# Constants, weight loads and a store of ones moved within the seam between two stages of a graph network

## The chip, the cores and the metric

The kernel runs on one core of a Trainium2 chip. The metric is the device time of one execution in microseconds. The core has five engines that run side by side, each through its own queue in order: PE (matrix multiply, into the accumulation banks of PSUM), DVE (vector work), ACT (scalar functions), POOL (general vector work) and SP, which here only issues transfers. The transfers themselves run on 16 DMA engines.

## The reference

There are 16 graphs of 1024 nodes with 128 features, an adjacency matrix of 1024 x 1024 for each, and a node mask. Two layers follow each other, each as `x = layernorm(x + layer(x))`.

- Layer 0 is a gated graph network: four times `m = adj^T (h W)`, then a GRU cell of `m` and `h`.
- Layer 1 first dilates the adjacency: row after row, every `sf`-th neighbour of a node with more than ten neighbours is removed, in both directions. Then three SAGE convolutions follow, each `out = (adj_d x / deg) Wr + x Wx + b`, rows divided by their norm, relu, and batch norm over all graphs and nodes. The three outputs, side by side, are multiplied by `Wl`.

## The kernel before, in words

The kernel runs in stages: the GRU and the dilation interleaved (classes `Gated` and `FixPoint`), then class `Sage` with `first` (first convolution, graph by graph), `second`, `third` and `last`. The batch norms join them, so that a convolution is only begun when the one before has seen all graphs. The adjacency kept by the dilation is stored as a bf16 matrix of what is not removed (`e_nr`), and layer 0's result as `e_sum`, both in device memory. The seam of this case lies between the first stage and `first`.

In `first` a graph is worked on in 16 slots. `slot(b, t)` runs slot `t` with two graphs in hand: the current one `b`, for the convolution, and the next one `n = b + 1`, whose adjacency is being formed. `b` starts at -1: in the sixteen slots of this lead-in turn nothing is convolved, and graph 0 is only prepared. A slot holds:

- `unit(n, t)`: one block of the dilated, transposed adjacency. PE adds up a half row of `p_nr` (L1482) and four blocks each of `p_a` (L1488) and `p_nr` (L1489) in PSUM, and ACT writes the result to `p_at` (L1490). Units 0 to 7 read the adjacency tiles a0 to a3 of the graph, units 8 to 15 read a4 to a7.
- `pack` (L1497): POOL turns the unit of the slot before into bytes, which SP stores for the later stages (`at8`, L1685 and L1677).
- `check` (L1506): DVE passes once over an adjacency tile, counts entries that aren't 0 or 1, and leaves bf16 values in the tile's lower halves. It stands in slots 4, 5, 10 and 11 for tiles 4 to 7 of graph `n`, and in slots 12 to 15 for tiles 0 to 3 of the graph after it.
- `norm_stats`, `norm` (L1527), `split_x` (L1405, L1406), `turn_x` (L1411): the layer norm of graph `n`'s rows `p_s`, their parts of high and low precision `p_xh` and `p_xl`, and their transpose.
- For graph `b`: `agg` (L1561, the adjacency times features, 8 matmuls each in slots 0, 1, 3, 4 and again 9, 10, 12, 14), `degrees`, `out_first` in slots 5 and 7 (with the weights `wr`, `wx` and the bias row `r6`), `scale_rows`, `rows`, and the stores.

The order of work on PE, DVE, ACT, POOL and SP is the written order of the program within a stage (a manual schedule), so a slot's place in the code is its place in every queue. SP issues all loads of this stage: `load_a` (L1458, one tile of 512 KB), `load_nr` (L1466, half a graph, 1 MB), `load_s` (L1472). In a slot they stand first: for the graph after `n`, `load_nr` in slots 4 and 6, `load_s` in slot 7, `load_a` of tiles 0 to 3 in slots 8 to 11, and of tiles 4 to 7 in slots 0 to 3 of the next turn. SP waits when the buffer isn't free: `p_a0` and `p_a1` hold four tiles each, `p_nr0` and `p_nr1` one graph each.

Three functions are concerned. `load_given` issues twenty transfers: three pairs of SAGE weights (`wr` L1248, `wx` L1249), `wl` (L1250), ten vectors into `vr` (L1253) and the node mask three times into a working tile named `p_rh` (L1257). `constants` forms small constant tiles on DVE and two selects on POOL (L1272), a copy of the identity with its first row changed (`drop`, L1284), and a tile of ones which SP stores three times as rows of `rho` (L1290). Identity copy, ones and a junk tile lie in a working tile named `p_rl`. `first_weights` takes the weights through PE once, `wr` with `drop` (L1297), splits the bias into `r6` (L1330 to L1337), and casts the node mask into `mask48` (L1303). `constants` runs at the end of slot (-1, 9), `first_weights` at the end of slot (0, 1). The tiles `wr2` and `wxp` get their values only between `first` and `second`; `mask48` is read in `last`.

Of the kernel before, what the change touches and what calls it, by code (L numbers as in the profile page):

```python
# [8 lines left out]
F32 = mybir.dt.float32  # L9
BF = mybir.dt.bfloat16  # L10
# [11 lines left out]
P = 128  # L22
B = 16
N = 1024
C = 128
NB = N // P
# [576 lines left out]
def make_consts(tc, one, wk, ps, nodemask):  # L603
    nc = tc.nc
    ident = one.tile([P, P], F32, name="ident")
    make_identity(nc, ident)
    ident_b = one.tile([P, P], BF, name="ident_b")
    nc.vector.tensor_copy(ident_b, ident)
    one_col = one.tile([P, 1], BF, name="one_col")
    nc.vector.memset(one_col, 1.0)  # L610

    nm = wk.tile([B, N], F32, name="nm_in")
    nc.sync.dma_start(nm, nodemask)
    pm = ps.tile([P, NB, B], F32, name="nm_ps")
    for k in range(NB):
        nc.tensor.transpose(pm[:, k, :], nm[:, k * P:(k + 1) * P], ident[:B, :B])
    mask = one.tile([P, NB, B], F32, name="mask")
    nc.vector.tensor_copy(mask, pm)

    t = wk.tile([P, NB, B], F32, name="nm_t")  # L620
    nc.vector.tensor_scalar(t, mask, 0.0, 4106.0, op0=ALU.is_equal, op1=ALU.mult)
    first = one.tile([P, NB, B], BF, name="first")
    nc.vector.tensor_scalar(first, t, -10.0, None, op0=ALU.add)
    return {"ident": ident, "ident_b": ident_b, "one_col": one_col, "mask": mask, "first": first}
# [292 lines left out]
class Gated:  # L917
# [24 lines left out]
    def bank(self):  # L942
        return self.ps6.tile([P, HF], F32, name="h_g")
# [180 lines left out]
    def run(self, steps):  # L1124

        streams = [self.stream(s) for s in range(2)]
        first, second = streams
        first.load_x(first.b)
        for j in range(NB):
            first.load_adj(first.b, j)  # L1130
        self.load_weights()
        next(steps)
        first.begin_rows(first.b)
        self.prepare()
        second.load_x(second.b)
        for j in range(NB):
            second.load_adj(second.b, j)

        first.begin(0)
        for n in range(9):  # L1140
            next(steps)
        for b0 in range(0, B, 2):
            for l in range(L0):
                for s in range(2):
                    st, ot = streams[s], streams[1 - s]
                    self.layer(st, l, self.beside(st, ot, l, s, b0, steps))
        last = streams[1]
        for f in range(2):
            last.finish(f)
        for _ in steps:  # L1150
            pass
# [45 lines left out]
class Sage:  # L1197
# [61 lines left out]
    def constants(self):  # L1259

        nc, ident, K = self.nc, self.cst["ident"], 3 * B
        const = self.const
        self.one16 = const([1, 1], 1.0, "s_one16", F16)

        self.sel01 = const([10, 3, 6], 0.0, "s_sel01")
        for i in range(3):
            nc.vector.tensor_copy(self.sel01[:, i, 3:], ident[:10, 3 * i:3 * i + 1].to_broadcast([10, 3]))
        self.ones = const([6, P], 1.0, "s_ones", BF)
        nc.vector.tensor_add(self.part6, ident[:6, 0:3], ident[:6, 3:6])
        self.part48 = const([K, 3], 1.0, "s_part48")  # L1270
        for base, m in ((0, 1), (B - 1, -1)):
            nc.gpsimd.affine_select(self.part48, self.part48, pattern=[[-m * B, 3]], compare_op=ALU.is_ge,  # L1272
                                    fill=0.0, base=base, channel_multiplier=m)
        nc.vector.tensor_add(self.graph, ident[:K, :B], ident[:K, B:2 * B])
        nc.vector.tensor_add(self.graph, self.graph, ident[:K, 2 * B:K])
        nc.vector.memset(self.r6[:, C:], 0.0)
        work = self.wk.tile([P, NB, C], F32, name="p_rl", bufs=1)

        mask, junk = self.cst["mask"], work[:, 0, :].rearrange("p (a b) -> p a b", a=NB)
        nc.vector.scalar_tensor_tensor(junk, mask, 0.0, mask, op0=ALU.is_gt, op1=ALU.not_equal,  # L1280
                                       accum_out=self.bad[:, BAD - 1:BAD])

        drop = work[:, 1, :]
        nc.vector.tensor_copy(drop, ident)  # L1284
        nc.vector.memset(drop[:1, :], -1.0)
        nc.vector.memset(drop[:1, :1], 0.0)
        o = work[:B, 4:, :].bitcast(BF).rearrange("p a b -> p (a b)")
        nc.vector.memset(o, 1.0)
        for i in range(3):
            nc.sync.dma_start(self.rho[:, 3 + i, :], o)  # L1290
        self.drop = drop

    def first_weights(self):
        nc, ident = self.nc, self.cst["ident"]
        bank = lambda: self.ps1.tile([P, 4, P], F32, name="s_tr")[:, 0, :]
        w = bank()
        nc.tensor.matmul(w, self.drop, self.wr[:, 0, :], start=True, stop=True)  # L1297
        nc.vector.tensor_copy(self.wr[:, 0, :], w)
        v = bank()[:, :10]
        nc.tensor.transpose(v, self.vr, ident[:10, :10])  # L1300
        nc.vector.tensor_copy(self.vt, v)
        self.weights(0, bank()[:6, :])
        nc.vector.tensor_copy(self.mask48, self.m48)  # L1303

    def const(self, shape, v, name, dt=F32):
        t = self.one.tile(shape, dt, name=name)
        self.nc.vector.memset(t.bitcast(F32) if dt is FR else t, v)
        return t
# [106 lines left out]
    def first(self):  # L1415

        nc, tc, cst = self.nc, self.tc, self.cst
        with ExitStack() as c:
            pool = lambda name, **k: c.enter_context(tc.tile_pool(name=name, **k))

            self.atp = [pool("p_at0", bufs=1)]
            self.sp = pool("p_s", bufs=2)
            xp = pool("p_x", bufs=1)
            self.wk = pool("p_wk", bufs=2)
            self.atp.append(pool("p_at1", bufs=1))
            self.nrp, self.ap = [], []
            for i in range(2):
                self.nrp.append(pool(f"p_nr{i}", bufs=1))
                self.ap.append(pool(f"p_a{i}", bufs=4))
            self.ps1 = pool("p_ps1", bufs=1, space=PSUM)  # L1430
            self.ps2 = pool("p_ps2", bufs=2, space=PSUM)

            self.ps3 = pool("p_ps3", bufs=3, space=PSUM)
            c.enter_context(tc.manual_schedule(engines={ET.PE, ET.DVE, ET.Activation, ET.Pool, ET.SP}))
            self.g = {}
            self.load_nr(0, 0)
            for k in range(4):
                self.load_a(0, k)
            self.load_nr(0, 1)
            self.load_s(0)  # L1440
            for k in range(4, NB):
                self.load_a(0, k)
            self.load_given()
            self.eps = self.const([P, 1], 1e-5, "s_eps")
            self.less2 = self.const([P, 1], -2.0, "s_less2")

            self.xh = xp.tile([P, NB, C], FR, name="p_xh")
            self.xl = xp.tile([P, NB, C], FR, name="p_xl")
            for t, v in ((self.xh, 1.0), (self.xl, 0.0)):
                nc.vector.memset(t[:, :, :1].bitcast(F32), v)  # L1450
            for b in range(-1, B):
                for t in range(16):
                    self.slot(b, t)
# [146 lines left out]
    def slot(self, b, t):  # L1600

        nc, g, n = self.nc, self.g.get(b), b + 1
# [80 lines left out]
        if nxt:  # L1683
            if t == 10:
                nc.sync.dma_start(self.at8[n, 0], self.g[n]["b", 0])  # L1685
            if t == 13:
                nc.sync.dma_start(self.x1[n], self.g[n]["s"])
        if (b, t) == (-1, 9):
            self.constants()
        if (b, t) == (0, 1):  # L1690
            self.first_weights()
        if t == 1 and b >= 1:
            for f in range(2):
# [346 lines left out]
```

## Time and profile before

| | us |
|---|---|
| three runs | 2393.73, 2396.82, 2397.0 |
| span of the profiled execution | 2393.6 |
| PE busy in it | 2269.3 (95%) |
| DVE busy | 1924.3 (80%) |
| ACT busy | 1373.5 (57%) |
| POOL busy | 1014.7 (42%) |
| first transfer of the first SAGE stage issued at | 1316.73 |
| first unit's matmul at | 1328.39 |
| first aggregation at | 1366.89 |

Times in the text are microseconds from the start of the profiled execution. An engine's busy share says little by itself; what counts is which wait ended last at a given place. The granted TensorE clock is given as a share of full speed (0.98 over the whole span); its value in a stage matters where PE has stood still. "L1284" is line 1284 of the kernel, and names such as `p_a` are tiles, without their buffer numbers. The matmuls of a group overlap, so a group's time is from its first start to its last end.

### The profile page before, as it was taken

The numbers are of one execution on the slowest core, as the hardware profiler recorded it, in microseconds if no ns is written. First come the engines' busy times: TensorE is split into PE (matmuls) and PEld (weight loads), VectorE is DVE, ScalarE is ACT, GpSimd is POOL, SyncE is SP. The second block draws the span as 40 slices with busy tenths as digits, with TensorE's granted clock in tenths as the row PEclk, the third lists the DMA queues.
The fourth block names the chain that finished last, engine by engine and source line by source line (L and its number), as shares of the span: only waits on it lengthen the run. The fifth ranks groups of instructions, "written<-read, shape, count | busy, mean of one in ns | idle before, by whom it ended". The sixth has DMA issues, their size and how long they took to land.

```text
span 2393.6 us, 35727 instructions
## 1 busy us (share of the span) xinstructions
PE 2269.3 (95%) x11945; PEld 1561.1 (65%) x11945; DVE 1924.3 (80%) x4130; ACT 1373.5 (57%) x3209; POOL 1014.7 (42%) x963
## 2 busy tenths in 40 slices
PE   6999999999999999999999599999999889998987
PEld 4666555656556656656666377777777777776865
DVE  4998998989989989989899777877777466665876
ACT  3556565665565656565746466566666444545756
POOL 3235253353362543533622356666666344441001
PEclk9999999999999999999999799999999999999999
DMA  7337254364271553533630868777877366664414
GB/s 260 111 98 262 69 191 146 115 230 132 95 246 60 176 185 119 186 132 119 231 101 31 315 237 295 280 258 282 300 277 269 116 215 232 242 207 147 143 45 134
DMA packets 214394, 436.18 MB, mean 182 GB/s; under 512 B 59574, under 2 KB 80728, under 8 KB 214200
## 3 DMA queue, kind: packets, MB, share of 16 engines
q1 hardware_dynamic: 186756, 345.96, 41.9%
q0 software_dynamic: 23040, 83.90, 10.2%
q10 hardware_dynamic: 4400, 3.95, 0.5%
q8 instruction: 96, 1.57, 0.3%
q14 instruction: 102, 0.80, 0.1%
HBM read 324.49 MB, written 109.25 MB: 181 GB/s over the span
## 4 chain that ended last, share of the span: by engine, by line
PE 58%; DVE 16%; ACT 10%; DMA 9%; issue 4%; POOL 3%; SPq 0%; DVEq 0%; ACTq 0%; POOLq 0%
PE h_g L1092 15%; PE h_g L1080 12%; PE p_ag L1561 9%; DMA e_sum<-h_x 3%; DVE f_rank L735 3%; ACT s_junk L1389 3%; PE q_ag L1800 3%; PE p_u L1482 2%; PE p_u L1489 2%; PE p_u L1488 2%; DMA h_a<-in_adj_dram 2%; PE q_ob L1764 2%; PE s_tr L1411 1%; DVE s_o L1382 1%; PE u_p L1890 1%
## 5 line engine op out<-in xcount | busy, mean ns | idle before, releaser
L1092 PE MATMUL h_g<-h_h,h_wh 128*128 128x512 f32 x768 | 397.7, 599 | 3.4 <-DVE h_r L1105 3.3
L1092 PE MATMUL h_g<-h_ms,h_wi 128*128 128x512 f32 x768 | 392.2, 592 | 0.0
L1497 POOL CAST p_b<-p_at 128x512 uint8<-128x512 f32 x256 | 251.7, 1003 | 139.8 <-ACT p_at L1490 131.3
L735 DVE TENSOR_TENSOR_SCAN f_rank<-f_a,f_first,f_pd 128x1024 f16<-128x1024 f32 x128 | 299.1, 2342 | 3.3
L1080 PE MATMUL h_g<-h_a,h_hi 128*128 128x512 f32 x1024 | 284.8, 418 | 6.4 <-DMA h_a<-in_adj_dram 6.3
L1490 ACT ACTIVATE p_at<-p_u,s_less 128x512 fp32r<-128x512 f32 x256 | 175.7, 687 | 160.0 <-PE p_u L1489 155.1
L1092 PEld LDWEIGHTS h_g<-h_ms,h_wi 128*128 128x128 f32 x768 | 145.6, 190 | 183.9 <-issue 161.6
L1121 POOL TENSOR_TENSOR h_h<-h_zh,h_r 128x512 f32<-128x512 f32 x126 | 182.0, 1444 | 194.9 <-DVE h_r L1120 172.8
L1080 PE MATMUL h_g<-h_a,h_lo 128*128 128x512 f32 x1024 | 264.2, 395 | 0.0
L1080 PEld LDWEIGHTS h_g<-h_a,h_hi 128*128 128x128 f32 x1024 | 188.4, 188 | 71.0 <-issue 20.1
L863 DVE SCALAR_TENSOR_TENSOR f_nr<-f_u,f_q,f_a 128x1024 bf16<-128x1024 f16 x128 | 183.7, 1451 | 57.2 <-ACT f_u L912 50.6
L1115 POOL TENSOR_TENSOR h_zh<-h_z,h_h 128x512 f32<-128x512 f32 x63 | 80.4, 1276 | 323.8 <-ACT h_z L1111 323.8
L1080 PEld LDWEIGHTS h_g<-h_a,h_lo 128*128 128x128 f32 x1024 | 190.0, 188 | 39.3
L1506 DVE SCALAR_TENSOR_TENSOR p_a<-p_a 128x1024 bf16<-128x1024 f32 x128 | 209.4, 1674 | 3.1 <-DMA p_a<-in_adj_dram 3.1
L1092 PEld LDWEIGHTS h_g<-h_h,h_wh 128*128 128x128 f32 x768 | 129.1, 190 | 86.6 <-issue 67.3
L1389 ACT ACTIVATE s_junk<-s_o 128x128 bf16<-128x128 f32 x384 | 113.7, 298 | 109.3 <-DVE s_o L1382 109.3
L1083 ACT COPY h_ms<-h_g 128x512 f32<-128x512 f32 x128 | 73.7, 576 | 175.2 <-PE h_g L1080 131.2
L1108 ACT ACTIVATE h_r<-h_r,h_bi 128x512 f32<-128x512 f32 x128 | 92.3, 721 | 138.7 <-DVE h_r L1107 138.7
L1488 PE MATMUL p_u<-ident_b,p_a 128*128 128x128 bf16 x1024 | 144.7, 221 | 13.8 <-DMA p_a<-in_adj_dram 13.8
L909 ACT ACTIVATE f_u<-f_rank,f_q 128x128 f16<-128x128 f16 (+7 forms) x128 | 110.6, 867 | 75.2 <-DVE f_rank L849 75.2
L1489 PE MATMUL p_u<-ident_b,p_nr 128*128 128x128 bf16 x1024 | 144.7, 221 | 0.0
L1764 PE MATMUL q_ob<-s_wxp,q_xt 128*128 128x256 f32 x512 | 130.8, 399 | 0.0
(258 smaller groups left out, 4956.8 us busy)
## 6 DMA issues: line engine op xcount, KB each, us to landing
h_a<-in_adj_dram POOLq DMA_DIRECT2D x128, 512.0 KB, 7.4
p_a<-in_adj_dram SPq DMA_DIRECT2D x128, 512.0 KB
f_a<-in_adj_dram SPq DMA_DIRECT2D x124, 512.0 KB
e_nr<-f_nr SPq DMA_DIRECT2D x128, 256.0 KB
p_nr<-e_nr SPq DMA_DIRECT2D x32, 1024.0 KB
s_at<-p_b SPq DMA_DIRECT2D x32, 512.0 KB
s_ag<-s_ag SPq DMA_DIRECT2D x64, 256.0 KB
q_agi<-s_ag SPq DMA_DIRECT2D x32, 512.0 KB
```

What stands on the lines that cost most here:

```text
L735: nc.vector.tensor_tensor_scan(out, a, other[:, 0, 0:1].to_broadcast([P, N]), start, op0=ALU.add, op1=ALU.bypass)
L863: nc.vector.scalar_tensor_tensor(nr, self.us[g], self.q[:, 2, g:g + 1], self.a[g], op0=ALU.not_equal, op1=ALU.is_ge)
L1080: nc.tensor.matmul(pm[f], part[:, j, :], st.adj[j][:, half[f]], start=(j == 0 and n == 0), stop=(j == NB - 1 and n == 1))
L1092: nc.tensor.matmul(pg, lhs, rhs, start=(i == 0), stop=(i == len(mm) - 1))
L1121: aid.tensor_tensor(h, zh, r, ALU.subtract)
L1389: self.nc.scalar.activation(junk, o[:, i, :], AF.Square, accum_out=ss[:, i:i + 1])
L1488: nc.tensor.matmul(pu[:, i * P:(i + 1) * P], a[:, blk, 1], ib, start=False, stop=False)
L1489: nc.tensor.matmul(pu[:, i * P:(i + 1) * P], nr[:, k, blk], ib, start=False, stop=(i == 3))
L1497: self.nc.gpsimd.tensor_copy(g["b", f][:, j, :], g["at"][:, j, f * HF:(f + 1) * HF].bitcast(F32))
L1506: self.nc.vector.scalar_tensor_tensor(low, a, 0.0, a, op0=ALU.is_gt, op1=ALU.not_equal, accum_out=self.bad[:, c:c + 1])
L1561: self.nc.tensor.matmul(pa, hi[:, j, :], at[:, j, f * HF:(f + 1) * HF], start=(start and n == 0), stop=(stop and n == len(js) - 1))
L1764: nc.tensor.matmul(pb[:, i], g["xt"][:, f, blk], self.wxp, start=False, stop=(i % 2 == 1))
```

## The change

`constants` is called before the slots begin, and no longer at the end of slot (-1, 9). Its junk tile lies in `wxp`, its identity copy in `wr2`, its ones in the first 16 rows of `mask48`. Its stores of ones go to the end of slot (-1, 15). `load_given` is called at the end of slot (-1, 11), behind the loads of graph 1, and no longer before the slots. `first_weights` is called at the end of slot (0, 3), and no longer (0, 1).

```diff
     def constants(self):
...
-        work = self.wk.tile([P, NB, C], F32, name="p_rl", bufs=1)
-
-        mask, junk = self.cst["mask"], work[:, 0, :].rearrange("p (a b) -> p a b", a=NB)
+
+        mask, junk = self.cst["mask"], self.wxp[:, 0, :].rearrange("p (a b) -> p a b", a=NB)
...
-        drop = work[:, 1, :]
+        drop = self.wr2
         nc.vector.tensor_copy(drop, ident)
         nc.vector.memset(drop[:1, :], -1.0)
         nc.vector.memset(drop[:1, :1], 0.0)
-        o = work[:B, 4:, :].bitcast(BF).rearrange("p a b -> p (a b)")
-        nc.vector.memset(o, 1.0)
-        for i in range(3):
-            nc.sync.dma_start(self.rho[:, 3 + i, :], o)
-        self.drop = drop
+        nc.vector.memset(self.mask48[:B, :], 1.0)
 
     def first_weights(self):
...
-        nc.tensor.matmul(w, self.drop, self.wr[:, 0, :], start=True, stop=True)
+        nc.tensor.matmul(w, self.wr2, self.wr[:, 0, :], start=True, stop=True)
...
     def first(self):
...
-            self.load_given()
             self.eps = self.const([P, 1], 1e-5, "s_eps")
             self.less2 = self.const([P, 1], -2.0, "s_less2")
...
                 nc.vector.memset(t[:, :, :1].bitcast(F32), v)
+            self.constants()
             for b in range(-1, B):
                 for t in range(16):
                     self.slot(b, t)
...
     def slot(self, b, t):
...
-        if (b, t) == (-1, 9):
-            self.constants()
-        if (b, t) == (0, 1):
+        if (b, t) == (-1, 11):
+            self.load_given()
+        if (b, t) == (-1, 15):
+
+            for i in range(3):
+                nc.sync.dma_start(self.rho[:, 3 + i, :], self.mask48[:B, :])
+        if (b, t) == (0, 3):
             self.first_weights()
```

## The prediction

> **What bounds the kernel now.** I read four views in this order: the page's slices, the chain that ended last around the change, SP's own queue there, and the waits with the busy times by stage.
>
> The change touches one place: the seam between the GRU/dilation stage and the first SAGE pass. In the page's slices the seam is slice 23 (59.84 us each, so 1316 to 1376 us), the only one in which PE falls to 5 tenths. The chain says what ended last there (columns: start, us, what):
>
> ```profile
> 1320.67 12.89 DMA p_s<-e_sum
> ...
> 1344.23 5.27 DVE p_a L1506 x6
> 1350.88 5.23 DVE p_rl L1284
> 1356.62 0.92 DVE p_rl L1288
> 1359.84 6.85 DMA p_a<-in_adj_dram
> 1367.13 3.52 PE p_ag L1561 x8
> ```
>
> PE waits for graph 1's fourth adjacency tile. Its load was issued late because SP stood behind the stores of ones, which stood behind DVE's constants (L1284, L1288). SP's queue, in order of time:
>
> ```profile
> 1326.34 1.02 SPq L1248 DMA_DIRECT2D s_wr<-in_L_gnn_Wr_dram  x1
> 1328.52 0.33 SPq L1249 DMA_DIRECT2D s_wx<-in_L_gnn_Wx_dram  x1
> 1332.29 0.33 SPq L1248 DMA_DIRECT2D s_wr<-in_L_gnn_Wr_dram  x1
> ...
> 1344.56 1.24 SPq L1257 DMA_DIRECT2D p_rh<-in_nodemask_dram  x3
> 1345.84 0.97 SPq L1466 DMA_DIRECT2D p_nr<-e_nr  x2
> 1346.85 0.50 SPq L1472 DMA_DIRECT2D p_s<-e_sum  x1
> 1347.47 1.14 SPq L1458 DMA_DIRECT2D p_a<-in_adj_dram  x2
> 1357.56 1.25 SPq L1290 DMA_DIRECT2D s_rho<-p_rl  x3
> 1358.91 0.37 SPq L1458 DMA_DIRECT2D p_a<-in_adj_dram  x1
> ```
>
> Two delays stand in one queue: twenty weight loads from 1326.34 to 1345.84 ahead of everything of graph 1, then the stores of ones at 1357.56. The waits of 1290 to 1440 us give their prices, and the stages what the machine did meanwhile (span, PE, PEld, DVE, ACT, POOL busy, clock, DMA share, GB/s):
>
> ```profile
> PE p_u L1488 <- DMA p_a<-in_adj_dram: 13.8, 4, 6.1
> ...
> SPq L1290 <- DVE p_rl L1288: 8.9, 1, 8.9
> ...
> 1340.00:1347.00 7.00, 6.74 (x72) 5.19 (x70) 7.00 (x11) 5.67 (x11) 6.46 (x7) 0.90 0.26 69
> ...
> 1357.50:1366.70 9.20, 1.18 (x6) 0.39 (x6) 6.14 (x11) 0.00 (x0) 0.00 (x0) 0.50 0.76 248
> ...
> 1392.40:1426.10 33.70, 33.26 (x273) 26.22 (x273) 25.64 (x61) 20.82 (x50) 22.03 (x20) 1.00 0.76 281
> ```
>
> The DMA engines idle from 1340 to 1347 (69 GB/s) while small loads go out, and pay for it in 1357.5 to 1366.7, where PE has 1.18 us of work. From 1392.4 on a graph takes 33.7 us with PE busy 33.26: there the loop is PE's, and whatever shift the seam gives is carried to the end.
>
> **What the Trainium skill says.** "SBUF — State Buffer", section on the two separate sides: VectorE and GpSimd share a port pair as an exclusive lock, and an fp32 SBUF-to-SBUF copy takes it. The trace agrees: the 128x128 copy L1284 took 5.30 us and ended 0.1 us after POOL's last cast, and the same size without POOL beside it (L1323) takes 0.28:
>
> ```profile
> 1347.75 1.76 DVE L1506 SCALAR_TENSOR_TENSOR p_a<-p_a 128x1024 bf16<-128x1024 f32 x1
> ...
> 1350.80 5.30 DVE L1284 COPY p_rl<-ident 128x128 f32<-128x128 f32 x1
> ...
> 1346.57 3.37 POOL L1497 CAST p_b<-p_at 128x512 uint8<-128x512 f32 x2
> ...
> 1353.74 2.27 POOL L1497 CAST p_b<-p_at 128x512 uint8<-128x512 f32 x4
> ```
>
> "DMA: Bandwidth & Descriptors", section on the anatomy of one DMA: about 2 us fixed per DMA, mostly completion, so small transfers must overlap. Here the ten vectors and three mask rows go out 0.25 to 0.6 us apart with eight in flight, so each took under some 3 us, which agrees. "TensorE: Matmul & The Clock Gate", part 1: an idle window of about 3.4 us halves the clock. Here it shows 0.50 in the hole, and slot (0,0)'s eight matmuls take 3.76 us against 2.09 for the same eight at 1405.59.
>
> **Part 1: constants moved in front.** Today DVE is in them from 1349.43 to 1357.46, 8.03 us. Of these 5.30 is the locked copy. In front, POOL runs no elementwise work between 1322.6 and 1338.3, so the copy costs 0.28 and the group 8.03 - 5.30 + 0.28 = 3.0 us. They follow the two memsets of L1450 (1325.6). From there to 1333.59, where DVE waits for the first p_s tile, DVE has 8.0 us and uses 2.07 (three of 0.69): 5.9 us free for 3.0. If some fall ahead of the last GRU operations (L1121, L1058), p_u starts up to 3 us later. That is hidden too: after p_at of units 0 and 1 and the table load (done 1333.1) ACT waits 3.9 us for p_mv, which waits for p_s. Cost on the path 0, with 0 to 3 as bounds. POOL's two selects (0.59 us) go along, into idle time. What is gained is that DVE is out of the way at 1349.4.
>
> **Part 2: load_given moved behind graph 1's loads.** SP runs at most eight loads ahead: the 14th after the seam (second s_wr) waits for the 6th (p_nr), the 15th for the 7th (p_s, 1333.59), the 16th to 19th for the four a tiles (1336.48 to 1340.98). So the 12th to 14th become p_nr of graph 1 (two of 1 MB) and p_s (0.5 MB), issued at about 1326.4, 1328.5 and 1332.3, queued behind graph 0's tiles. They arrive in that order now, so I take it that graph 0 isn't slowed. Then a(1,0) to a(1,2): their buffers are free once unit (0,7) is through (1342.6) and checks 0 to 2 (1342.6). Then the byte store at8, which waits for POOL's pack of unit 7 (1348.2, the first of the two casts at 1346.57), then a(1,3) at about 1348.7. By volume: 2 + 0.5 + 2 + 0.5 MB = 5.24 million bytes after 1340.9, at the 415 GB/s seen before, are 12.6 us: a(1,3) lands at 1353.5 to 1354. It lands at 1366.7 today. **Gain at this point 12.7 to 13.2 us.**
>
> **Part 3: the twenty loads in their new place.** They are issued from 1349.1. The first seven wait in turn for the loads eight before, up to a(1,3) (1353.9); the other thirteen took 4.9 us (1340.98 to 1345.84): last at 1358.9. Then x1's store, the three of ones (1.25 us) and a(1,4) at about 1361.7: by chance the time at which it is issued now (1361.69). Landing about 1364.5, the last of the four about 1369.5; DVE's check needs the first at 1364 to 1370, PE the last in slot (0,8) at about 1376. p_nr and p_s of graph 2 follow by 1376, before slot (1,0). No cost, 2 us at the most.
>
> **Part 4: stores of ones from mask48.** Source ready since part 1, so SP no longer waits the 8.9 us. In return L1303's cast of the node mask into mask48 must wait for them (landed about 1363.6); DVE gets there at 1367 to 1370. Cost 0.
>
> **Part 5: first_weights from slot (0,1) to (0,3).** Same work, 1.6 us on PE (1373.81 to 1375.38) and a chain of 3.8 us on DVE. Its weights land by about 1360, PE arrives at about 1364. The row r6 must be ready for slot (0,5): one slot (2.7 us) and a unit (0.65) lie between, against 3.0 us from the first copy to r6: 0, at most 1.
>
> **Part 6: what takes the gap's place.** DVE's six checks (0,6) to (1,3) now run alone after 1357.46 (1.27 us each). Moved to 1349.5 they run beside POOL's remaining casts and alternate with them, 1.76 as above, one of 2.4 beside the split: about 11.5 us, to 1361, where uncontended they would end at 1357. norm_stats (2.2) then ends at 1363.3, the degree row and norms follow, first_weights finds DVE at 1366.7 where PE came at about 1364.6. That gives back about 2 us. Against it, PE stands still 2.5 us and not 16, so slots (0,0) and (0,1) may run warm: 1.6 + 0.6 us less. I take -2 for the first and 1 for the second.
>
> **Sum:** 12.9 - 2 + 1 = 12 us less, 2393.6 to 2381.6 in the profiled span. The runs shown are 2393.73 to 2397.0, median 2396.82; 12 off the median is 2385.
>
> **The rivals.**
> *Partial gain.* DVE beside POOL, or SP's small loads, end last in slots (0,1) to (0,6). For it: 1.76 against 1.27 us, and L1248's wait of 3.4 us. If the checks take 2.4 each (the worst seen) the end is 1364, three more lost, and with 2 us of late loads 5 to 8 us are left: 2389 to 2392. Against: PE has about 11 us of own work before it needs what DVE makes.
> *No change.* The loads queue but don't move earlier: graph 1's buffers in fact free late, or early p_nr takes bandwidth from p_s. Then a(1,3) still lands near 1366: 2395 to 2397. Against: p_nr of graph 1 is the first tile in its own pool, and the loads at 1321.55 had already waited for the dilation's last DVE instruction.
> *Slower.* PE takes its queue in order, so first_weights in slot (0,3) holds it until the last vector has landed. Place: twenty loads now stand between a(1,3) and that point. Price: 1 us for each us after 1364.6. They lasted 19.5 us when each waited for a large load; from 1349.1 that is 1368.6 plus landing, 5 lost. It decides against the change from 1377 on, 28 us for the twenty; at 33 us PE goes on at 1382.1, 17.5 lost against 12, and the time is 2402. Against: only seven have a large load eight places ahead.
>
> **How the numbers follow.** Forecast case 0.64 (2382 to 2388), a still warmer PE included; partial 0.22; no change 0.07; slower 0.07. Within 0.2% (4.8 us) is about what a measurement of this kernel can't tell from no change. Faster 0.86, same 0.07, slower 0.07. The range 2380 to 2392 holds the forecast and the partial case and leaves out the other two (0.14) and a tail; the forecast's own is 2382 to 2388.
>
> **What would show it.** Right: the a tile's 6.1 us wait on PE is gone and the fourth block of unit (1,0) starts at about 1354; DMA above 400 GB/s from 1340 to 1353; the copy of the identity at about 0.3 us before 1334; the checks of 1349 to 1361 at about 1.8 us. Wrong: a PE wait for s_wr or s_vr in slot (0,3), a(1,3) issued after 1352, the constants beside POOL's work, or p_s of graph 0 landing after 1335.

## The result and the profile after

The changed kernel takes 2385.58 us (median of four runs, 2382.49 to 2386.91), the kernel before 2396.60 in the same series: 0.9955 of its time, interval 0.9938 to 0.9972. That is 11.0 us less, against a forecast of 12. The profiled spans are 2393.6 and 2385.2, only 8.4 apart: the profiled execution of the changed kernel was the slowest of its four.

In the chain that ended last (start, us, what), the piece of 6.85 us for graph 1's tile and DVE's constants ahead of it are gone:

```profile
1321.20 12.50 DMA p_s<-e_sum
...
1344.49 4.40 DVE p_a L1501 x5
...
1354.52 5.76 DVE p_a L1501 x7
1360.29 0.77 DVE p_st L1510 x4
...
1365.27 1.12 DVE p_s L1522 x4
1368.80 2.98 PE p_ag L1556 x8
```

From 1354.52 to 1366.4 the chain now runs over DVE, but for 0.8 us of ACT: the checks, the statistics and the norm of graph 1. SP's queue (start, us, line, transfer) shows the new order and how the large loads are spread:

```profile
1326.65 4.34 SPq L1461 DMA_DIRECT2D p_nr<-e_nr  x2
1332.48 5.60 SPq L1467 DMA_DIRECT2D p_s<-e_sum  x1
1343.48 1.29 SPq L1453 DMA_DIRECT2D p_a<-in_adj_dram  x3
1348.56 0.33 SPq L1680 DMA_DIRECT2D s_at<-p_b  x1
1349.00 0.37 SPq L1453 DMA_DIRECT2D p_a<-in_adj_dram  x1
1349.42 0.71 SPq L1248 DMA_DIRECT2D s_wr<-in_L_gnn_Wr_dram  x1
...
1359.00 1.65 SPq L1688 DMA_DIRECT2D s_rho<-s_mask  x3
1360.76 1.31 SPq L1453 DMA_DIRECT2D p_a<-in_adj_dram  x3
```

Graph 1's `p_nr` and `p_s` are issued from 1326 to 1338 and no longer at 1345, its fourth tile at 1349.00 and no longer at 1358.91. The waits of 1290 to 1440, then the stages (span, PE, PEld, DVE, ACT, POOL busy, clock, DMA share, GB/s):

```profile
PE p_u L1483 <- DMA p_a<-in_adj_dram: 2.3, 1, 2.3
...
1340.00:1347.00 7.00, 6.66 (x62) 5.42 (x60) 7.00 (x12) 5.13 (x10) 5.57 (x8) 0.74 1.04 397
1357.50:1366.70 9.20, 7.00 (x52) 4.93 (x50) 8.36 (x33) 3.12 (x6) 6.77 (x8) 1.00 0.78 237
1392.40:1426.10 33.70, 33.22 (x273) 26.22 (x273) 25.73 (x64) 20.81 (x50) 22.41 (x21) 1.00 0.78 282
```

PE's 13.8 us of waits for tiles have become 2.3. The DMA engines move 397 GB/s where they moved 69, and in the old hole PE works 7.00 us of 9.20 where it worked 1.18. The later loop is as it was.

To compare executions I use one length, the seam: from the start of the first memset of `first` (`s_eps`) to the first aggregation of slot (0,9). It is 79.91 us before (1312.50 to 1392.41) and 68.65 after (1312.90 to 1381.55), 11.3 less. The gain is kept: the last `p_oa` product of the first convolution comes 577.1 us after that memset before, and 566.2 after, 10.9 less. A seam is read from one profiled execution; two more of the changed kernel, below, gave 68.91 and 68.01.

### The profile page after: what moved, and what is told of

Same layout as the page of the kernel before. It is cut to its first block, busy times and chain, and to the rows that moved or that the text cites. A ratio compares the mean times of both kernels' runs of the same rounds, so it can differ in the third digit from the quotient of the medians.

```text
span 2385.2 us, 35712 instructions
## 1 busy us (share of the span) xinstructions
PE 2272.1 (95%) x11928; PEld 1566.9 (66%) x11945; DVE 1921.6 (81%) x4130; ACT 1373.1 (58%) x3209; POOL 1018.7 (43%) x963
## 4 chain that ended last, share of the span: by engine, by line
PE 56%; DVE 17%; ACT 11%; DMA 8%; issue 4%; POOL 2%; SPq 0%; DVEq 0%; ACTq 0%; POOLq 0%
PE h_g L1092 14%; PE h_g L1080 11%; PE p_ag L1556 9%; DVE f_rank L735 3%; DMA e_sum<-h_x 3%; ACT s_junk L1384 3%; PE q_ag L1799 2%; DMA h_a<-in_adj_dram 2%; PE p_u L1483 2%; PE p_u L1484 2%; PE p_u L1477 2%; PE q_ob L1763 2%; PE s_tr L1406 1%; PE u_p L1889 1%; DVE s_o L1377 1%
## 5 line engine op out<-in xcount | busy, mean ns | idle before, releaser
L1492 POOL CAST p_b<-p_at 128x512 uint8<-128x512 f32 x256 | 257.1, 1024 | 123.2 <-ACT p_at L1485 123.2
```

The source lines that it names most:

```text
L1492: self.nc.gpsimd.tensor_copy(g["b", f][:, j, :], g["at"][:, j, f * HF:(f + 1) * HF].bitcast(F32))
```

## The experiments

Each expectation was written before its run. Theory: the tile's wait was set by two things in a row, SP's weight loads in front and DVE's locked copy in front of the stores. Rival: one of the two made nearly all of it.

**The loads moved, the constants left.** All of the change but `constants`, which is back at the end of slot (-1, 9) with its stores:

```diff
-            self.constants()
             for b in range(-1, B):
...
-        if (b, t) == (-1, 15):
+        if (b, t) == (-1, 9):
+            self.constants()
             for i in range(3):
                 nc.sync.dma_start(self.rho[:, 3 + i, :], self.mask48[:B, :])
```

> The changed kernel, but with the constants and the stores of ones back at the end of slot (-1, 9); only the weight loads (and first_weights) are moved. Theory (two delays in series in SP's queue, the later one decides): the first three quarters of graph 1's loads go out early, but the third a tile still waits on SP for the stores of ones, which wait for the 5.3 us copy; a(1,2) is issued near 1358.9 and a(1,3) near 1359.8, now into idle DMA engines, so it lands near 1363 to 1364. Gain against before 2.5 to 3.5 us, time 2393 to 2394. Rival (the weight loads in front are the main piece, the DMA engines' idle 7 us is what is won): 7 us or more, time 2389 or less.

2392.0 us, 0.9987 of before (0.998 to 0.9994); seam 75.29. The gain of 3.7 is a little more than the 2.5 to 3.5 expected, and it came by another path: the copy was not slow here, and the third tile went out at 1354.16 and not near 1358.9. First DVE, then SP, then the chain, then two stages:

```profile
1350.95 0.21 DVE L1283 COPY s_wr<-ident 128x128 f32<-128x128 f32 x1
...
1352.53 4.93 DVE L1500 SCALAR_TENSOR_TENSOR p_a<-p_a 128x1024 bf16<-128x1024 f32 x1
...
1352.62 1.43 SPq L1685 DMA_DIRECT2D s_rho<-s_mask  x3
...
1355.18 6.32 DMA p_a<-in_adj_dram
...
1344.00:1348.00 4.00, 3.76 (x45) 2.84 (x43) 4.00 (x7) 3.67 (x7) 3.09 (x2) 1.00 0.95 369
1348.00:1353.00 5.00, 2.76 (x33) 1.98 (x31) 4.60 (x22) 3.10 (x6) 4.54 (x8) 0.99 0.04 15
```

Here the copy took 0.21 us, just ahead of POOL's row of casts (from 1351.16), and the check after it took 4.93. Even so, SP stood behind the stores' source until 1352.6, and with all that was issued before already in, the DMA engines stood nearly empty (15 GB/s) for 5 us; the last two tiles were issued after it.

**The constants moved, the loads left in front.**

```diff
                 self.load_a(0, k)
+            self.load_given()
             self.eps = self.const([P, 1], 1e-5, "s_eps")
...
-        if (b, t) == (-1, 11):
-            self.load_given()
```

> The changed kernel, but with the weight loads back in front of the slots; only the constants, their stores and first_weights are moved. Theory: graph 1's loads start at 1345.8 as before and are then bound by volume (5.24 million bytes at 0.4 per us are 13 us), so a(1,3) lands near 1359.5 to 1360 in place of 1366.7; DVE's checks end near 1361, before PE needs them. Gain 6 to 7.5 us, time 2389 to 2391. Rival (weight loads the main piece): 4 us or less, time 2392.5 or more.

2391.85 us, 0.9985 (0.9976 to 0.9993); seam 77.65. Expected was 6 to 7.5 less, measured 3.9. Chain and stages:

```profile
1349.43 13.51 DMA p_a<-in_adj_dram
...
1346.00:1348.00 2.00, 1.89 (x26) 1.41 (x24) 2.00 (x3) 1.73 (x4) 2.00 (x3) 1.00 0.67 195
1348.00:1363.00 15.00, 3.01 (x26) 1.51 (x25) 7.93 (x12) 2.08 (x4) 8.57 (x9) 0.62 1.02 385
```

The tile was issued at 1349.43, which is 37.4 us after the seam's start against 36.1 in the changed kernel, and landed 13.5 us later. Two terms were missing from the expectation: the DMA engines were at 195 GB/s until 1348, and the store of `x1` (0.5 MB, issued 1350.91) shared them with the tile. 11 half-megabyte units (5.77 million bytes) at 385 GB/s are 15.0 us: 1348 to 1363. Here volume ends last, not issue. A gain of 4 us or less was the rival's mark for this run; what speaks against the rival is that the loads alone didn't give its 7 us either.

**One instruction of the kernel before: the identity copy on ACT.**

```diff
-        nc.vector.tensor_copy(drop, ident)
+        nc.scalar.copy(drop, ident)
```

> The kernel before with one line changed: the copy of the identity in the constants runs on ACT in place of DVE, so that it doesn't take part in the lock with POOL. Theory: DVE's 5.3 us copy is on the path; the stores of ones go out near 1352.5, a(1,3) near 1355, volume-bound as in the constants-alone kernel: a(1,3) lands near 1359.5 to 1361. Gain 5 to 7 us, time 2390 to 2391.5. Rival (the copy only looks long, DVE would wait elsewhere, for instance the stores wait for POOL or the memset takes the lock's time): 0 to 1 us, time 2396.

2392.11 us, 0.9985 (0.9978 to 0.9991); seam 75.46. 3.6 us less; 2390 to 2391.5 was expected. DVE, SP, chain:

```profile
1353.69 5.04 DVE L1506 SCALAR_TENSOR_TENSOR p_a<-p_a 128x1024 bf16<-128x1024 f32 x1
...
1353.79 1.26 SPq L1290 DMA_DIRECT2D s_rho<-p_rl  x3
...
1348.46 9.61 DMA p_s<-e_sum
1358.13 6.31 DMA p_a<-in_adj_dram
```

On ACT the copy took 0.31 us with a cast of POOL beside it. DVE's 5 us did not go away, they passed to the next check; but that stands behind the stores' source, so SP's stores came at 1353.79. The tile was then held by the transfer eight places ahead of it, `p_s`, which landed at 1358.1.

So each of the three ways to take away one delay gives 3.6 to 3.9 us (2.3 to 4.6 by the seam of its one profile), and taking away both gives 11.0, in another series. The rival falls: with one delay gone something else sets nearly the same end, issue (constants left, or the copy on ACT) or volume (loads left). The move of `first_weights` was part of both halves; by itself it wasn't tried.

**The changed kernel again, as a yardstick for three kernels on one chip.**

> The changed kernel once more, as the yardstick for the three kernels beside it. Both theories: 2384 to 2387, 9 to 11 us under the kernel before.

2384.63 us, 0.9948 (0.9935 to 0.9962), 12.8 us under the kernel before; seam 68.91.

**Four checks later.** The prediction held that DVE beside POOL gives back about 2 us. Tiles 0 to 3 of graph 1 are checked in slots (0,6), (0,8), (0,9), (0,10):

```diff
-            if t >= 12:
+            if t >= 12 and now:
                 self.check(n + 1, t - 12)
+            if b == 0 and t in (6, 8, 9, 10):
+                self.check(1, (6, 8, 9, 10).index(t))
```

> The changed kernel, with DVE's four checks of graph 1's first tiles moved from slots (-1, 12) to (-1, 15) into slots (0, 6), (0, 8), (0, 9) and (0, 10). Theory (after the change DVE's checks beside POOL's casts end last in slots (0, 2) to (0, 4)): norm_stats ends near 1355 in place of 1362.4, PE meets first_weights without the wait for s_rdeg, at most 1 us is left for the round trips, and slot (0, 9)'s first aggregation starts 1.5 to 3 us earlier than in the changed kernel (1381.55 there). Time 1 to 3 us under the changed kernel. Rival (PE is held by the round trips of first_weights and by the late a tile, not by DVE's checks): 0 to 0.5 us.

2384.82 us, 0.9948 (0.9935 to 0.9962); seam 68.19, 0.7 shorter than the yardstick's, and nothing in the time: the rival's figure, not the theory's 1 to 3. DVE was out of the way as expected, its statistics done at 1355.3. But PE reached `first_weights` 52.6 us after the seam's start instead of 53.3 in the yardstick: the late tile (3.3 us of wait) and the half clock held PE nearly as long. Slot (1,3) then lost that again, by a wait for `p_rl` and an aggregation at lowered clock (the yardstick's takes 2.09):

```profile
1404.11 0.25 PE L1549 MATMUL s_tr<-s_one,p_rl 1*128 1x1 f16 x4 [1.72 <-ACT p_rl L1542]
...
1405.33 3.29 PE L1556 MATMUL p_ag<-p_at,p_xl 128*128 128x512 f32 x8
```

**The fourth tile ahead of the byte store.** `load_a(1, 2)` and `load_a(1, 3)` both in slot (-1, 10), so that the tile isn't behind `at8`:

```diff
-            if 8 <= t < 12:
+            if 8 <= t < 12 and (now or t < 10):
                 self.load_a(n + 1, t - 8)
+            if (b, t) == (-1, 10):
+                self.load_a(1, 2)
+                self.load_a(1, 3)
```

> The changed kernel, with the load of graph 1's fourth a tile issued ahead of the byte store of graph 0 in SP's queue. Both: it is issued near 1346 and not 1349.0, PE's last block of unit (1, 0) starts near 1353 and not 1354.3. Theory (DVE's checks end last afterwards): PE waits for DVE in slot (0, 3) as before, slot (0, 9) starts within 0.5 us of the changed kernel's, time the same within 1 us. Rival (the a tile still sets the seam): 1.3 us less.

2385.0 us, 0.9946 (0.9932 to 0.9959); seam 69.41. PE's queue, with the wait and its releaser in brackets:

```profile
1353.07 2.07 PE L1556 MATMUL p_ag<-p_at,p_xh 128*128 128x512 f32 x8
...
1365.73 0.49 PE L1292 MATMUL s_tr<-s_wr,s_wr 128*128 128x128 f32 x2 [0.64 <-DMA p_a<-in_adj_dram]
1367.19 0.27 PE L1295 MATMUL s_tr<-ident,s_vr 10*128 10x10 f32 x1 [0.97 <-DVE s_wr L1293]
1369.46 3.76 PE L1556 MATMUL p_ag<-p_at,p_xl 128*128 128x512 f32 x8
```

As the theory said, nothing was won. The first aggregation starts 3.0 us earlier than in the yardstick (39.4 us after the seam's start against 42.4) and at full clock, but PE comes to `first_weights` only 1.2 us earlier (52.1 against 53.3), after 2.5 us of wait for ACT's `p_rl`: ACT had stood 6.4 us for the statistics that DVE forms behind its checks. And the half clock (3.76 us) strikes four slots later. PE and DVE reach this point nearly together; freeing one of them alone gave nothing.

**Both at once, with the weights back in slot (0,1).**

```diff
-        if (b, t) == (0, 3):
+        if (b, t) == (0, 1):
             self.first_weights()
```

> The two edits together, and first_weights back at the end of slot (0, 1). Theory: DVE is free from 1355 on, so the chain of first_weights runs as soon as PE comes to it near 1359.5; the weights' last vector lands near 1359, which may cost up to 1 us; slot (0, 9) starts 3 to 5 us earlier than in the changed kernel. Time 2380.5 to 2383. Rival (the weights' loads then hold PE at slot (0, 1)): no better than the checks moved alone, 2383 to 2385.

2385.51 us, 0.9947 (0.9933 to 0.996); seam 66.33. The seam is 2.6 shorter, the time isn't (2380.5 to 2383 was expected). In slot (0,6) PE waits for `s_rdeg`:

```profile
1372.05 0.66 PE L1406 MATMUL s_tr<-ident,p_s 128*128 128x128 f32 x4 [1.87 <-DVE s_rdeg L1551]
```

DVE, which makes it, had stood 0.84 us at the cast into `mask48`, until the stores of ones from that tile had landed; in the changed kernel it comes there later and isn't held. After the wait PE ran at half clock (0.50 from 1373.3 to 1377.9). Slot (1,3) again waits 1.8 us for `p_rl`, and the next aggregation takes 3.30, as with the four checks moved alone: in slots (0,6) to (0,10) they seem to push DVE's later work back by about as much as they freed before. The version with two moved bears that out.

**Two checks later, and none.** As the last kernel, but with only tiles 2 and 3 moved (slots (0,8) and (0,9)), and the cast into `mask48` moved from `first_weights` to slot (0,6); and the same with all checks in their place. The changed kernel ran beside them.

```diff
-            if t >= 12:
+            if t >= 12 and (now or t < 14):
                 self.check(n + 1, t - 12)
+            if b == 0 and t in (8, 9):
+                self.check(1, t - 6)
...
+        if (b, t) == (0, 6):
+            nc.vector.tensor_copy(self.mask48, self.m48)
```

> The changed kernel as the yardstick beside the next two: 2384 to 2387 by every theory.

> The changed kernel with the fourth a tile ahead of the byte store, first_weights at the end of slot (0, 1), its cast of the node mask at the end of slot (0, 6), and only two of the four checks moved, into DVE's idle times of slots (0, 8) and (0, 9). Theory (PE and DVE are in balance over slots (0, 0) to (1, 3); moving all four checks pushed DVE into graph 1's turn, which cost 1.8 us of waiting and 1.2 us of cold clock there; two fit into idle times): slot (0, 9) starts 2 to 3 us earlier than in the changed kernel and slot (1, 3) shows no wait over 1 us for p_rl. Time 1.5 to 3 us under the changed kernel. Rival (any DVE work that is put off comes back in full): within 1 us of it.

> The same, with all four checks left in their places. Theory: first_weights in slot (0, 1) then meets DVE still in its checks until about 1361, PE waits 2 to 4 us there, the clock falls, and slot (0, 9) starts no earlier than in the changed kernel (within 1 us). Time within 1.5 us of it. Rival (the checks don't hold PE, the place of first_weights did): slot (0, 9) 2 us earlier or more.

| | us | of before | seam |
|---|---|---|---|
| changed kernel | 2386.05 | 0.9955 (0.9942 to 0.9969) | 68.01 |
| two checks later | 2382.51 | 0.9939 (0.9926 to 0.9953) | 65.94 |
| checks in place | 2387.43 | 0.9961 (0.9949 to 0.9974) | 69.77 |

PE's wait at `first_weights`, first with two checks moved, then with none:

```profile
PE s_tr L1295 <- DVE s_wr L1293: 2.6, 1, 2.6
...
PE s_tr L1295 <- DVE s_wr L1293: 5.9, 1, 5.9
```

Two checks out of DVE's queue are 3.3 us less of wait and 3.8 of seam, and slot (1,3) waits only 0.4. These two versions differ in nothing but the two checks, and five of the six runs with two moved lie under all six with none moved; the medians are 4.9 apart. The version with two moved has the lowest median of all, 3.5 us under the changed kernel beside it (1.5 to 3 was expected). Those two intervals overlap, so the size of that step is not settled; the seam, 2.1 shorter, is in the direction of it.

## Why the prediction was right

**Part 1, constants in front.** As predicted, off the path: they ran from 1327.34 to 1331.7, before DVE's wait of 2.0 us for `p_s`. Some came ahead of the GRU's last L1058, which waited for ACT anyhow. The copy:

```profile
1330.04 0.22 DVE L1283 COPY s_wr<-ident 128x128 f32<-128x128 f32 x1
...
1333.72 0.87 DVE L1510 BATCH_NORM_STATS2 p_st<-p_s 128x6 f32<-128x128 f32 x4 [2.02 <-DMA p_s<-e_sum]
```

**Part 2, the loads of graph 1.** The sum by volume said 1353.5 to 1354 for the fourth tile; the block that needs it started at 1354.28, and the first aggregation at 1354.44 instead of 1366.89. That is 12.45 us earlier, and 12.85 when each is counted from the start of its seam (12.7 to 13.2 predicted):

```profile
1354.28 0.29 PE L1483 MATMUL p_u<-ident_b,p_a 128*128 128x128 bf16 x1 [2.34 <-DMA p_a<-in_adj_dram]
1354.44 3.43 PE L1556 MATMUL p_ag<-p_at,p_xh 128*128 128x512 f32 x8
...
1366.65 0.23 PE L1295 MATMUL s_tr<-ident,s_vr 10*128 10x10 f32 x1 [0.96 <-DVE s_wr L1293]
...
1368.56 3.22 PE L1556 MATMUL p_ag<-p_at,p_xl 128*128 128x512 f32 x8
```

The halves tried alone bear the sum out: only with both delays gone do the bytes start early and the stores no longer hold up the tile's issue. One sign failed. The DMA engines were to move over 400 GB/s from 1340 to 1353; they moved 397 until 1347, 408 until 1350, and then 314. Nor was volume all: with the tile ahead of the byte store the first aggregation came 39.4 us after the seam's start, against 41.5 here. What slowed the last 3 us wasn't traced; the weight loads went out from 1349.42.

**Parts 3 to 5.** a(1,4) was issued at 1360.76 (1361.7 predicted), and PE waits nowhere over 0.3 us for tiles 4 to 7. SP did not wait for the ones' source, and DVE was not held at the cast into `mask48` (1369.80). PE never waited for `s_wr`'s or `s_vr`'s load in slot (0,3), so the slower rival had nothing to stand on.

**Part 6, what takes the gap's place.** The checks did alternate with POOL's casts and ended at 1360.3 (1361 predicted); `first_weights` found DVE at 1366.32 (1366.7):

```profile
1349.69 1.76 DVE L1501 SCALAR_TENSOR_TENSOR p_a<-p_a 128x1024 bf16<-128x1024 f32 x1
...
1356.14 2.47 DVE L1501 SCALAR_TENSOR_TENSOR p_a<-p_a 128x1024 bf16<-128x1024 f32 x1
...
1346.83 8.22 POOL L1492 CAST p_b<-p_at 128x512 uint8<-128x512 f32 x5
```

From slot (0,0) to slot (0,9) PE needs 27.11 us instead of 25.52: 1.6 given back, against a net 1 in the sum (2 for DVE, less 1 for the clock). Both terms were mis-sized. PE's waits of over 0.2 us in this stretch are 2.72 us against 1.91 before, so they cost 0.8 more, where the sum had 2 for DVE: what PE now waits in slot (0,3) is partly not waited any more in slot (0,6) (1.26 us for `s_rdeg` before, 0.26 after). The clock gives 0.9 us (slot (0,0) to (0,1) takes 3.92 instead of 4.83) and takes back 1.1, since slot (0,4) takes 3.22 instead of 2.11, at a granted clock of 0.62, after three waits of 0.6 to 1.0 us. The remaining 0.6 us lies just ahead of that slot: PE stands 0.23 us with no releaser shown, and the unit there takes 0.82 us where it took 0.42 before. So the clock took about 0.6 where the prediction had it give 1: after 2.5 us of standing still PE was to run warm, and slot (0,0) took 3.43.

How the loss is made up differs between executions of the same kernel. In the two other profiles of it this stretch took 26.52 and 26.48 us, so 1.0 was given back; slot (0,0) took 3.76 and 2.89, slot (0,4) ran at full clock (2.10), and slot (0,6) waited 1.1. The net of 1 was therefore right to within 0.6 us, but its two terms were both too large and of opposite sign. That they made up for each other was luck.

The partial rival named the right mechanism, DVE beside POOL, and put it too high: it needed 2.4 us for each check; one of the six was that long. That both DVE and PE arrive at this point together, so that neither alone is worth anything, the prediction did not say; the checks, the tile and the weights had to be moved to see it.

## What to carry to other kernels

Where two delays stand in one in-order queue of transfers, each removed alone may show little (here a third) of what both give: sum the bytes that are left after the issue times, and take the later of issue and volume. Work that is put off from a balanced place comes back in the next turn unless the new place has room for it: four checks moved gave nothing; two, with the tile and the weights moved as well, ended 3.5 us lower, not yet clear of noise. And when an instruction is slow because of a lock, taking it away may only pass the wait to its successor, as it did twice here; ask who waits for the successor.

## What the runs showed of the hardware

**The shared port of DVE and POOL.** The Trainium skill, "SBUF — State Buffer", section on the two separate sides, says that the pair is held for one whole instruction and the loser blocks. The runs show a coarser picture. One DVE instruction that came upon POOL's row of casts stood until the whole row (casts and a split) was through: 5.30 us for the copy in the kernel before, 4.93 and 5.04 for a check where the copy had slipped by or was gone. The copy ended 0.1 us after the row's last cast, the checks 1.15 us after it, and alone they take 0.22 and 1.27. A row of checks already running instead took turns with POOL, 1.76 each. And in one execution of the changed kernel five checks ran on at 1.35 to 1.46 us each while one of POOL's casts, 0.6 by itself, took 7.86; its DVE and POOL queues:

```profile
1355.21 1.35 DVE L1501 SCALAR_TENSOR_TENSOR p_a<-p_a 128x1024 bf16<-128x1024 f32 x1
1356.40 0.17 DVE L1501 DVE_READ_ACCUMULATOR p_a<-p_a 128x1 f32 x1
1356.40 1.39 DVE L1501 SCALAR_TENSOR_TENSOR p_a<-p_a 128x1024 bf16<-128x1024 f32 x1
...
1349.58 12.30 POOL L1492 CAST p_b<-p_at 128x512 uint8<-128x512 f32 x5
```

That execution's seam was 68.01 against 68.65, so the sum was nearly the same. What decides between the three is open; it wasn't tried.

**The clock.** "TensorE: Matmul & The Clock Gate", part 1, gives an idle window of about 3.4 us for the drop to half clock. Here less was enough. The table has holes in PE's work and how long the next aggregation took, which takes 2.07 to 2.11 us at full clock:

| PE stood still, us | in | next aggregation, us |
|---|---|---|
| 0.9 | tile ahead, slot (0,0) | 2.07 |
| 1.7 | four checks later, slot (1,3) | 3.29 |
| 2.3 | changed kernel, slot (0,0) | 3.43 |
| 2.6 | two checks later, `first_weights` | 3.14 |
| 3.2 | yardstick, slot (0,0) | 3.76 |
| 5.9 | checks in place, `first_weights` | 2.53 |

The measurement decides: the holes of 1.7 us and more were all followed by a lowered clock. What they cost on top doesn't grow with their length: after 5.9 us the half clock (0.50 from 1364 to 1368) fell mostly on small matmuls ahead of the aggregation. Nor need it be one hole: slot (0,4) of the changed kernel, after three short waits, took 3.22. What sets the moment of the drop stays open.
